# Pair products on one core: x in 16 KB rows, and four half stores in place of nine loads on GpSimd's DMA queue

## The chip, the cores and the metric

The kernel runs on one core of a Trainium2 chip. The metric is the time of one execution on the device in microseconds (us); it is given as the median of several runs. The core has a matrix engine (PE), a vector engine (DVE), a scalar engine (ACT), GpSimd (POOL) and a sync engine (SP); ACT, POOL and SP are used here only to issue DMA transfers, and all transfers run on the core's 16 DMA engines, numbered 0 to 15.

## The reference

The input holds 4096 samples of 32 fields with 64 numbers each. For each of the 496 pairs of fields (i, j) with i < j, field i is multiplied by a 64 x 64 matrix of that pair, and the result is multiplied element by element with field j. Everything is float32.

```python
i_idx, j_idx = np.triu_indices(32, k=1)
vi = inputs[:, i_idx, :]                       # (4096, 496, 64)
vj = inputs[:, j_idx, :]
vdotw = jnp.einsum('bpd,pde->bpe', vi, W)      # W: (496, 64, 64)
y = (vdotw * vj).reshape(4096, -1)
```

The output is 4096 x 31744 float32, 520 MB. The input x has 33.6 MB, the matrices W 8.1 MB.

## The kernel before, in words

**Tiling.** The samples are cut into 8 chunks of 512 (`NC` chunks of `BANK` columns). x is laid out transposed: a pair of fields p (16 of them, `NPR`) fills 128 partitions (two fields of 64) by 512 samples. Four pairs make a group (`GROUP`); the tile `x` holds all four groups of one chunk, 8 KB per partition and group. W stays in SBUF for the whole run.

**Steps.** `steps_of` lists the 124 steps of a chunk. A step (p, q) takes two PSUM banks: PE makes two blocks of 128 x 512 there (L190; the first step of a group, with q None, is four smaller matmuls, L181), and one DVE instruction multiplies them by the x rows of q and writes the two finished blocks into the ring (L207; L200 for the special step). Steps with p in group 0 come first, 55 of them, and begin with q in group 0, then group 1 from step 7, group 2 from step 23, group 3 from step 39; then follow 39 steps with p in group 1, 23 with p in group 2 and 7 with p in group 3. Over 8 chunks that makes 992 steps and 1984 blocks of 256 KB.

**Ring.** Finished blocks go into a ring of three slots of 20, 18 and 18 blocks (`SLOTS`). One filling of a slot is a turn; there are 107. When a slot is full, SP stores it (L216), 4608 or 5120 KB in 128 rows of 36 or 40 KB; in the first three turns each half is stored by itself. The slot may be filled again when its store has landed. The output tensor in DRAM has 128 long rows, one per partition, so the rows of one store lie 1984 x 2 KB = 4.06 MB apart.

**x loads.** Group g of the next chunk is loaded after the last step of the present chunk with p in g (`last`, L221 to L223), since nothing reads the old group after that. A load has 1 MB in 128 rows of 8 KB. Of the 32 loads, 23 are issued by ACT (L131).

**Nine loads on GpSimd.** The nine listed in `LIGHT_LOADS` are issued by GpSimd through `load_beside` (L105). A transfer from SP or ACT over 128 partitions gives each of the 16 DMA engines 8 rows. `load_beside` instead splits the load into two: rows 0 to 119 in 15 shares of 8 rows, which start at engine 5 and so leave out engine 4 (`LIGHT`), and rows 120 to 127 in two shares of 4 rows on two engines from `PAIRS_FROM`. [...] Before each of the two parts, `from_engine` therefore issues a tiny load into a tile `nudge` over as many engines as are needed to move on to the wanted one. The shares are kept apart in DRAM by pads of 16 numbers (`PAD`), so that the transfer has an outer dimension of 15 or 2. All of these stand in program order on GpSimd, which does nothing else.

Of the kernel before, what the change touches and what calls it, by code (L numbers as in the profile page):

```python
# [8 lines left out]
F32 = mybir.dt.float32  # L9
ALU = mybir.AluOpType  # L10

P = 128
BANK = 512
BANKS = 8

GROUP = 4
W_STEPS = [8, 16, 24, 32, 44]
SLOTS = [20, 18, 18]

DMA_ENGINES = 16  # L20
LIGHT = 4
LIGHT_LOADS = [(1, 0), (2, 0), (3, 0), (3, 2), (4, 0), (5, 0), (6, 0), (6, 2), (7, 0)]
PAIRS_FROM = [5, 7, 9, 11, 13, 15, 1, 6, 8]
HEAD = P // DMA_ENGINES
REST = HEAD // 2
PAD = 16


def steps_of(NPR):

    steps = []
    for g in range(0, NPR, GROUP):
        steps.append((g, None))
        for h in range(g, NPR, GROUP):
            for p in range(g, g + GROUP):
                steps += [(p, q) for q in range(max(h, p + 1), h + GROUP)]
    return steps


def row_half(p, i):  # L40

    return (i + p) % 2
# [10 lines left out]

def x_loads(B, NPR):

    return [(c, g) for c in range(B // BANK) for g in range(NPR // GROUP)]


def load_size(load, D):

    pads = (DMA_ENGINES + 1) * PAD if load in LIGHT_LOADS else 0
    return P * GROUP * BANK + pads


@with_exitstack
def pair_bilinear_kernel(
    ctx: ExitStack,
    tc: tile.TileContext,
    x: bass.AP,
    w: bass.AP,  # L70
    out: bass.AP,
    B: int,
    F: int,
    D: int,
):

    nc = tc.nc
    NC = B // BANK
    NPR = F // 2
    steps = steps_of(NPR)  # L80
    blocks = 2 * len(steps) * NC

    const = ctx.enter_context(tc.tile_pool(name="const", bufs=1))
    psum = ctx.enter_context(tc.tile_pool(name="ps", bufs=1, space=bass.MemoryType.PSUM))

    nudges = [const.tile([DMA_ENGINES, 16], F32, tag=f"nudge{i}", name=f"nudge{i}") for i in range(2)]
    cursor = 0

    def from_pool(out, in_):

        tc.keep_in_program_order(nc.gpsimd.dma_start(out=out, in_=in_))  # L91

    def from_engine(e):

        nonlocal cursor
        k = (e - cursor) % DMA_ENGINES
        if k:
            nudge = nudges[e == LIGHT + 1]
            from_pool(
                nudge[:k].rearrange("p (h c) -> p h c", h=2)[:, :, :4],  # L100
                x[: k * 8].rearrange("(p h c) -> p h c", p=k, h=2),
            )
        cursor = e

    def load_beside(at, xt, n_row, lap):  # L105

        nonlocal cursor
        most = DMA_ENGINES - 1
        for e, k, rows, p in (
            (PAIRS_FROM[lap], 2, REST, most * HEAD),  # L110
            (LIGHT + 1, most, HEAD, 0),
        ):
            from_engine(e)
            n = rows * n_row
            lines = x[at : at + k * (n + PAD)].rearrange("(k c) -> k c", k=k)
            from_pool(xt[p : p + k * rows], lines[:, :n])
            at += k * (n + PAD)
            cursor = (e + k) % DMA_ENGINES

    xbuf = const.tile([P, NPR * BANK], F32, tag="x", name="x")  # L120
    loads = x_loads(B, NPR)

    def load_x(load):

        at = sum(load_size(before, D) for before in loads[: loads.index(load)])
        n = GROUP * BANK
        xt = xbuf[:, ts(load[1], n)]
        if load in LIGHT_LOADS:
            load_beside(at, xt, n, LIGHT_LOADS.index(load))
        else:  # L130
            nc.scalar.dma_start(out=xt, in_=x[at : at + P * n].rearrange("(p c) -> p c", p=P))  # L131

    for g in range(NPR // GROUP):
        load_x((0, g))
    w_sb = const.tile([P, len(steps) * P], F32, tag="w", name="w")
    done = 0
    for n in W_STEPS:
        cols = slice(done * P, (done + n) * P)
        nc.sync.dma_start(out=w_sb[:, cols], in_=w[:, cols])
        done += n  # L140

    pring = psum.tile([P, BANKS * BANK], F32, tag="pring", name="pring")
    bank = 0

    def take_banks(n):

        nonlocal bank
        got = pring[:, bank * BANK : (bank + n) * BANK]
        bank = (bank + n) % BANKS
        return got  # L150

    ring = ctx.enter_context(tc.tile_pool(name="ring", bufs=1))
    made = base = stored = 0
    room = 0
    turn = -1

    def x_of(p, h=None):

        rows = slice(None) if h is None else slice(h * D, (h + 1) * D)
        return xbuf[rows, ts(p, BANK)]  # L160

    def strided(ap, step):

        return bass.AP(ap.tensor, ap.offset, [ap.ap[0], [step, 2], ap.ap[1]])

    for c in range(NC):
        for s, (p, q) in enumerate(steps):
            pm = take_banks(2)
            if made == base + room:
                turn += 1  # L170
                base, room = made, SLOTS[turn % len(SLOTS)]
                tag = f"slot{turn % len(SLOTS)}"
                osb = ring.tile([P, room * BANK], F32, tag=tag, name=tag)
            a = (made - base) * BANK
            for k in range(2):
                if q is None:
                    for h in range(2):
                        pair = p + 2 * k + h
                        m = row_half(pair, 2 * pair)
                        o = row_half(pair, 2 * pair + 1)  # L180
                        nc.tensor.matmul(  # L181
                            pm[o * D : (o + 1) * D, ts(k, BANK)],
                            w_sb[m * D : (m + 1) * D, s * P + k * D : s * P + (k + 1) * D],
                            x_of(pair, m),
                            start=True,
                            stop=True,
                        )
                else:
                    m = row_half(p, 2 * p + k)
                    nc.tensor.matmul(  # L190
                        pm[:, ts(k, BANK)],
                        w_sb[m * D : (m + 1) * D, ts(s, P)],
                        x_of(p, m),
                        start=True,
                        stop=True,
                    )
            if q is None:
                for h in range(2):
                    rows = slice(h * D, (h + 1) * D)
                    nc.vector.tensor_tensor(  # L200
                        strided(osb[rows, a : a + BANK], BANK),
                        strided(pm[rows, :BANK], BANK),
                        strided(x_of(p + 1 - h, h), 2 * BANK),
                        ALU.mult,
                    )
            else:
                nc.vector.tensor_tensor(  # L207
                    strided(osb[:, a : a + BANK], BANK),
                    strided(pm[:, :BANK], BANK),
                    strided(x_of(q), 0),  # L210
                    ALU.mult,
                )
            made += 2
            half = turn < len(SLOTS) and made - base == (room // 2 + 1) // 2 * 2
            if half or made in (base + room, blocks):
                nc.sync.dma_start(  # L216
                    out=out[:, stored * BANK : made * BANK],
                    in_=osb[:, (stored - base) * BANK : (made - base) * BANK],
                )
                stored = made  # L220
            last = s + 1 == len(steps) or steps[s + 1][0] // GROUP != p // GROUP  # L221
            if last and c + 1 < NC:
                load_x((c + 1, p // GROUP))  # L223


# [53 lines left out]
```

## Time and profile before

| | |
|---|---|
| median of 10 runs | 1316.0 us (1313.98 to 1317.82) |
| the profiled execution | 1316.78 us |
| its span, first to last instruction | 1314.6 us |
| bytes moved by DMA | 562.41 MB, of them 520.09 MB written to DRAM |
| stores of 4608 KB, SP | 68, median 24.8 us from issue to landing |
| stores of 5120 KB, SP | 35, median 24.4 us |
| x loads of 1024 KB, ACT | 23, median 18.5 us |
| x loads of 960 KB, GpSimd | 9, median 27.9 us |
| the rest of these, 64 KB, GpSimd | 9, median 12.7 us |
| nudges, GpSimd | 18 |

The profile is of one execution. Busy times are sums over an engine's instructions; idle time of an engine that isn't the bottleneck costs nothing. In the queue list, q1 carries what SP issues (stores and W), q10 what ACT issues, q0 what GpSimd issues, and q8 and q14 carry the engines' own instructions from DRAM. The time from issue to landing includes what stood in the queue ahead of the transfer. A packet is one row of a transfer[...].

### The profile page before, as it was taken

What the parts mean: (1) busy time and instruction counts of PE and PEld (TensorE: products, weight loads), DVE (VectorE), ACT (ScalarE), POOL (GpSimd) and SP (SyncE); (2) the same over time, 40 slices, a digit from 0 to 9 for tenths busy, and PEclk for the clock granted to TensorE, in tenths of its full rate; (3) what the DMA queues carried; (4) which work ended last, traced back from release to release, by engine and by line L of the source; (5) the groups of instructions that cost most, each with busy time, mean ns of one, the idle gap of its engine ahead of it and who ended that gap; (6) DMA issues with size and microseconds to landing.
All of it is one profiled execution on the core that took longest, in us unless ns stands there. A gap on an engine that the chain in (4) does not pass through costs nothing.

```text
span 1314.6 us, 9765 instructions
## 1 busy us (share of the span) xinstructions
PE 1133.3 (86%) x4096; PEld 337.9 (26%) x4096; DVE 1170.9 (89%) x1024; POOL 20.7 (2%) x40
## 2 busy tenths in 40 slices
PE   7988889898798887999889888798988988889991
PEld 2222222222222222222222222222222222222220
DVE  6998989999899987999889999799998989889993
POOL 0000000000000000000000000000000000000000
PEclk9999999999899999999889999899988989999996
DMA  9999999999999999999999999999999999999998
GB/s 391 431 433 431 430 436 432 432 432 428 437 430 433 430 429 427 429 428 432 431 432 428 433 426 431 433 432 417 436 426 429 436 425 434 427 434 431 430 435 354
DMA packets 22507, 562.41 MB, mean 428 GB/s; under 512 B 3648, under 2 KB 3648, under 8 KB 3776
## 3 DMA queue, kind: packets, MB, share of 16 engines
q1 hardware_dynamic: 16560, 528.23, 93.5%
q10 hardware_dynamic: 3312, 24.12, 4.4%
q0 software_dynamic: 2592, 9.45, 1.8%
q8 instruction: 32, 0.52, 0.1%
q14 instruction: 11, 0.09, 0.0%
HBM read 41.69 MB, written 520.09 MB: 427 GB/s over the span
## 4 chain that ended last, share of the span: by engine, by line
DMA 65%; DVE 31%; PE 1%; issue 1%; DVEq 0%
DMA out_dram<-slot 64%; DVE slot L207 29%; DVE slot L200 2%; PE pring L190 1%; DMA x<-in_x_dram 1%; PE pring L181 0%; DVEq L207 0%; DVEq L269 0%; DVEq L200 0%
## 5 line engine op out<-in xcount | busy, mean ns | idle before, releaser
L190 PE MATMUL pring<-x,w 64*128 64x512 f32 x3840 | 1072.2, 657 | 146.3 <-DVE slot L207 106.7
L207 DVE TENSOR_TENSOR slot<-pring,x 128x1024 f32<-128x1024 f32 x960 | 1095.2, 1213 | 106.5 <-DMA out_dram<-slot 101.6
L190 PEld LDWEIGHTS pring<-x,w 64*128 64x128 f32 x3840 | 322.5, 194 | 896.2 <-DVE slot L207 753.6
L200 DVE TENSOR_TENSOR slot<-pring,x 64x1024 f32<-64x1024 f32 x64 | 77.9, 1217 | 14.8 <-PE pring L181 11.5
L181 PE MATMUL pring<-x,w 64*64 64x512 f32 x256 | 63.5, 615 | 9.3 <-DMA x<-in_x_dram 7.6
L181 PEld LDWEIGHTS pring<-x,w 64*64 64x64 f32 x256 | 15.4, 135 | 53.9 <-DVE slot L207 27.2
L91 POOL DMA_DIRECT2D x<-in_x_dram x18 | 10.5, 585 | 1022.6 <-PE pring L190 1022.6
L91 POOL DMA_DIRECT2D nudge<-in_x_dram x18 | 10.1, 562 | 0.9 <-POOLq L265 0.9
L265 POOL MEMSET const-float32-0.0<- 128x1 f32 x1 | 0.1, 98 | 0.2 <-issue 0.2
L265 POOL MEMSET const-bfloat16-1.0<- 128x1 bf16 x1 | 0.1, 101 | 0.0
L265 POOL MEMSET const-uint8-127<- 128x1 uint8 x1 | 0.1, 99 | 0.0
L265 POOL MEMSET const-float32-1.0<- 128x1 f32 x1 | 0.1, 98 | 0.0
## 6 DMA issues: line engine op xcount, KB each, us to landing
out_dram<-slot SPq DMA_DIRECT2D x68, 4608.0 KB, 24.8
out_dram<-slot SPq DMA_DIRECT2D x35, 5120.0 KB, 24.4
x<-in_x_dram ACTq DMA_DIRECT2D x23, 1024.0 KB, 18.5
out_dram<-slot SPq DMA_DIRECT2D x4, 2560.0 KB, 22.2
x<-in_x_dram POOLq DMA_DIRECT2D x9, 960.0 KB, 27.9
out_dram<-slot SPq DMA_DIRECT2D x2, 2048.0 KB, 23.0
w<-in_w_dram SPq DMA_DIRECT2D x1, 2816.0 KB, 25.3
w<-in_w_dram SPq DMA_DIRECT2D x1, 2048.0 KB, 23.1
```

The lines of the kernel that those rows point to most:

```text
L91: tc.keep_in_program_order(nc.gpsimd.dma_start(out=out, in_=in_))
L181: nc.tensor.matmul(pm[o * D : (o + 1) * D, ts(k, BANK)], w_sb[m * D : (m + 1) * D, s * P + k * D : s * P + (k + 1) * D], x_of(pair, m), st ...
L190: nc.tensor.matmul(pm[:, ts(k, BANK)], w_sb[m * D : (m + 1) * D, ts(s, P)], x_of(p, m), start=True, stop=True,)
L200: nc.vector.tensor_tensor(strided(osb[rows, a : a + BANK], BANK), strided(pm[rows, :BANK], BANK), strided(x_of(p + 1 - h, h), 2 * BANK), A ...
L207: nc.vector.tensor_tensor(strided(osb[:, a : a + BANK], BANK), strided(pm[:, :BANK], BANK), strided(x_of(q), 0), ALU.mult,)
L265: nc = bacc.Bacc("TRN2", target_bir_lowering=False, num_devices=1)
```

## The change

Four things change together.

1. x is loaded for two groups at once, 2 MB in 128 rows of 16 KB, except for the first two loads of chunk 0, which stay at one group each. `x_loads` now lists (chunk, first group, end group). For a later chunk, groups 0 and 1 are loaded after the last step with p in group 1, and groups 2 and 3 after the last step with p in group 3.
2. ACT issues all 17 x loads. `LIGHT_LOADS`, `PAIRS_FROM` and `load_beside` are gone, and so are the pads in x.
3. In turns 18, 45, 71 and 98 (`LIGHT_TURNS`) the slot is stored in two halves. The first, 10 blocks, is issued by GpSimd through `store_beside`: partitions 0 to 119 in 15 shares from engine 5 on, and partitions 120 to 127 in k shares from engine e on, with (e, k) from `REST_ON`: engines 7 and 8; 15, 0, 1 and 2; 15 and 0; 1 and 2. The second half, 10 or 8 blocks, is issued by SP.
4. The output in DRAM is no longer 128 long rows. Each store writes one contiguous region, partition after partition; the shares of the four GpSimd stores have pads of 16 numbers between them. The host puts the blocks in order.

```diff
-LIGHT_LOADS = [(1, 0), (2, 0), (3, 0), (3, 2), (4, 0), (5, 0), (6, 0), (6, 2), (7, 0)]
-PAIRS_FROM = [5, 7, 9, 11, 13, 15, 1, 6, 8]
+LIGHT_TURNS = [18, 45, 71, 98]
+REST_ON = [(7, 2), (15, 4), (15, 2), (1, 2)]
 HEAD = P // DMA_ENGINES
-REST = HEAD // 2
+MOST = DMA_ENGINES - 1
 PAD = 16
...
 def x_loads(B, NPR):
-    return [(c, g) for c in range(B // BANK) for g in range(NPR // GROUP)]
+    loads = [(0, 0, 1), (0, 1, 2), (0, 2, 4)]
+    for c in range(1, B // BANK):
+        loads += [(c, 0, 2), (c, 2, 4)]
+    return loads
+
+def stores_of(blocks):
+    stores = []
+    made = turn = 0
+    while made < blocks:
+        room = SLOTS[turn % len(SLOTS)]
+        half = (room // 2 + 1) // 2 * 2
+        cuts = [half, room - half] if turn < len(SLOTS) or turn in LIGHT_TURNS else [room]
+        for i, n in enumerate(cuts):
+            n = min(n, blocks - made)
+            if n:
+                light = LIGHT_TURNS.index(turn) if i == 0 and turn in LIGHT_TURNS else None
+                stores.append((made, n, light))
+                made += n
+        turn += 1
+    return stores
+
+def store_parts(store):
+    at, n, light = store
+    if light is None:
+        return [(0, 1, P)]
+    e, k = REST_ON[light]
+    return [(MOST * HEAD, k, HEAD // k), (0, MOST, HEAD)]
...
-    def load_beside(at, xt, n_row, lap):
+    def store_beside(at, osb, light):
         nonlocal cursor
-        most = DMA_ENGINES - 1
-        for e, k, rows, p in (
-            (PAIRS_FROM[lap], 2, REST, most * HEAD),
-            (LIGHT + 1, most, HEAD, 0),
-        ):
+        n = osb.shape[-1]
+        for e, (p, k, rows) in zip((REST_ON[light][0], LIGHT + 1), store_parts((0, n // BANK, light))):
             from_engine(e)
-            n = rows * n_row
-            lines = x[at : at + k * (n + PAD)].rearrange("(k c) -> k c", k=k)
-            from_pool(xt[p : p + k * rows], lines[:, :n])
-            at += k * (n + PAD)
+            m = rows * n
+            lines = out[at : at + k * (m + PAD)].rearrange("(k c) -> k c", k=k)
+            from_pool(lines[:, :m], osb[p : p + k * rows])
+            at += k * (m + PAD)
             cursor = (e + k) % DMA_ENGINES
...
-        if load in LIGHT_LOADS:
-            load_beside(at, xt, n, LIGHT_LOADS.index(load))
-        else:
-            nc.scalar.dma_start(out=xt, in_=x[at : at + P * n].rearrange("(p c) -> p c", p=P))
+        n *= g1 - g0
+        xt = xbuf[:, g0 * GROUP * BANK : g0 * GROUP * BANK + n]
+        nc.scalar.dma_start(out=xt, in_=x[at : at + P * n].rearrange("(p c) -> p c", p=P))
...
-            half = turn < len(SLOTS) and made - base == (room // 2 + 1) // 2 * 2
-            if half or made in (base + room, blocks):
-                nc.sync.dma_start(
-                    out=out[:, stored * BANK : made * BANK],
-                    in_=osb[:, (stored - base) * BANK : (made - base) * BANK],
-                )
-                stored = made
+            at, n, light = stores[0]
+            if made == at + n:
+                part = osb[:, (at - base) * BANK : (made - base) * BANK]
+                if light is None:
+                    nc.sync.dma_start(
+                        out=out[stored : stored + P * n * BANK].rearrange("(p c) -> p c", p=P),
+                        in_=part,
+                    )
+                else:
+                    store_beside(stored, part, light)
+                stored += store_size(stores.pop(0))
             last = s + 1 == len(steps) or steps[s + 1][0] // GROUP != p // GROUP
-            if last and c + 1 < NC:
-                load_x((c + 1, p // GROUP))
+            for load in loads:
+                if last and load[0] == c + 1 and load[2] == p // GROUP + 1:
+                    load_x(load)
```

`store_size` gives the number of elements that a store takes in DRAM, its pads included. The matmuls and the DVE instructions are the same, in the same order.

## The prediction

> **What bounds the kernel now.** I read the page's busy shares, slices and queues first, then the chain of waits, the groups, the waits, a table of windows, and last the DMA activity of the final 35 us.
>
> ```profile
> span 1314.6 us, 9765 instructions
> PE 1133.3 (86%) x4096; PEld 337.9 (26%) x4096; DVE 1170.9 (89%) x1024; POOL 20.7 (2%) x40
> DMA  9999999999999999999999999999999999999998
> DMA packets 22507, 562.41 MB, mean 428 GB/s; under 512 B 3648, under 2 KB 3648, under 8 KB 3776
> q1 hardware_dynamic: 16560, 528.23, 93.5%
> q10 hardware_dynamic: 3312, 24.12, 4.4%
> q0 software_dynamic: 2592, 9.45, 1.8%
> q8 instruction: 32, 0.52, 0.1%
> q14 instruction: 11, 0.09, 0.0%
> DMA 65%; DVE 31%; PE 1%; issue 1%; DVEq 0%
> L207 DVE TENSOR_TENSOR slot<-pring,x 128x1024 f32<-128x1024 f32 x960 | 1095.2, 1213 | 106.5 <-DMA out_dram<-slot 101.6
> ```
>
> DVE and PE are near the span, yet DVE's idle time ends on a store 101.6 us long: it waits for ring slots. The chain is 65% store DMA and only then DVE. The windows table says how full the DMA is (columns: window, then busy time and count of PE, PEld, DVE, POOL, then granted clock, DMA share, GB/s):
>
> ```profile
> 35.00:100.00 65.00, 58.69 (x210) 17.54 (x210) 60.18 (x54) 2.25 (x4) 0.95 1.01 433
> 100.00:500.00 400.00, 349.94 (x1280) 103.38 (x1276) 363.94 (x319) 6.75 (x12) 0.97 1.00 431
> 900.00:1290.00 390.00, 347.22 (x1256) 103.24 (x1252) 359.52 (x316) 4.01 (x7) 0.96 1.00 431
> 1290.00:1315.00 25.00, 0.00 (x0) 0.00 (x0) 2.23 (x2) 0.00 (x0) 0.52 0.75 322
> ```
>
> From 35 to 1290 us no DMA engine has a gap, so only three things can shorten the kernel: fewer bytes or packets, fewer stretched packets, or a tail in which the 16 engines stop together. The tail, in 40 slices of 0.875 us from 1280 to 1315 us:
>
> ```profile
> DMA  9879699699599798998999979999895735320000
> GB/s 590 379 337 590 295 463 548 295 463 506 253 590 426 342 613 346 407 445 365 510 421 421 562 328 421 421 431 431 346 477 225 328 169 225 150 94 37 19 0 0
> ```
>
> It fades over eight slices, 7 us. The packet records behind these views (start, duration, size, queue) make this exact: an engine's next packet starts 3 to 4 ns before its last one ends, so records link into 16 chains. By where those chains stop, the first engine ends 7.1 us before the last, and the mean 3.7 us before it. Perfect balance would be worth 3.7 us.
>
> Who is late can be told from the same chains. Each of the 32 instruction packets (q8, 16 KB, every 40 us) holds one engine 0.92 us and stretches that engine's next packet by 0.40 us: 1.32 us together. They return to the same engine every eighth time, so eight engines pay 4 x 1.32 = 5.3 us each and eight none. The chains that carry 12 instead of 8 rows of a GpSimd load name the engines: those paying are 5, 6 and 9 to 14. Engine 3 carries most of q14's 8 KB packets (about 4 us, an estimate from their 0.31 us plus a similar stretch). One chain has no rows of the GpSimd loads, so it is engine 4; its large packets take 1378 to 1396 ns where all others take 1364, and 30 ns x 847 such packets is 25 us over the run. Engine 4 is slow, and the nine GpSimd loads spare it 9 x 8 rows x 305 ns = 22.0 us.
>
> [...] the 18.5 us of a 1 MB x load agree: 8 rows x (305 + 1360) = 13.3 us and 5.2 us fixed.
>
> **The change, part by part.** Time per packet from link to link: 8 KB 305, 16 KB 607, 20 KB 757, 36 KB 1360, 40 KB 1510 ns, 4 B 6 ns.
>
> *x in 16 KB rows.* 4096 rows x 305 = 1249.3 us become 256 x 305 + 1920 x 607 = 1243.5; over 16 engines -0.36 us. Small packets: GpSimd's 36 DMAs left 1440, the new 16 leave about 640 (32 each plus nudges), ACT's completions fall by 96; 900 x 6 ns / 16 = -0.34 us. Four more turns cut in half: 512 rows x 4 ns / 16 = +0.13 us. Sum -0.57 us.
>
> *Later loads.* Groups 0-1 are now asked for after step 94 of 124, first read 30 steps on, PE four steps sooner: 26 x 1.21 = 31 us. Groups 2-3 are asked for at a chunk's end and first read (by DVE) at step 23: 28 us. A 2 MB load needs 8 x (607 + 1360) + 5.2 = 20.9 us: hidden. The longest ACT load of before took 31.2 us; if that recurs DVE stalls some 6 us, but two stores (12 us each) stand queued whenever DVE gets a slot and one is left when it has filled it, so the engines stay busy; beyond 12 us each us counts. ACT queues nothing but these loads.
>
> *Light stores.* In turns 18, 45, 71 and 98 GpSimd issues nudge, rest, nudge and 15 shares; SP issues the second half. GpSimd waits for DVE with nothing but its own later DMAs behind it, and SP loses one wait. Eight light rows per engine, about eight small packets between, alternate with queued SP rows: 16 x 1.36 + 8 x 0.757 + 5 = 33 us to land, against 24.8 for a whole store. SP's rows are pushed back at most 6 us; the same bytes flow, the 12 us of backlog covers it, and DVE gains back 12.1 - 11.4 = 0.7 us per turn over 26 turns. Cost zero, up to +1 us at each if the cover is thinner.
>
> *Balance.* The light stores spare engine 4 by 4 x 8 x 757 = 24.2 us. The rests fall on 7, 8 (4 + 4 rows, 6.1 us) and 15, 0, 1, 2 (2 + 4 rows, 4.5 us), the very engines without instruction packets. Extra work per engine, us:
> Before: 6 and 9: 5.3 + 8 rows x 0.305 = 7.7; 5, 10 to 14: 6.5; 7, 8: 2.4; 15, 0, 1, 2: 1.2; 3: 4; 4: 25.4 - 22.0 = 3.4. Mean 4.5, most 7.7: the last is 3.2 behind the mean (3.7 measured, so the count holds to 0.5).
> After: 5, 6, 9 to 14: 5.3; 7, 8: 6.1; 15, 0, 1, 2: 4.5; 3: 4; 4: 1.2. Mean 4.9, most 6.1: 1.2 behind.
> Gain 2.0 us; between 0 (the remaining scatter replaces it) and 2.5.
>
> *Stretched packets.* While GpSimd's x loads ran in the second half, packets beyond their usual times add 33 engine-us, and 15 ACT loads 11; on ACT the nine would cost about 7. Saved up to 26 / 16 = 1.6 us, or nothing if it hangs on addresses, which all change. I take 0.6.
>
> *Output layout.* Rows that stood 3.9 MB apart become contiguous. Before shows no contiguous store, but contiguous x loads run at full packet speed: I take 0. The pads of the first light store (17 x 64 B) put every later row 64 B or more off a 256 B boundary. [...] In before, x rows after the first light load are off by 64 B too and take 309 ns, as aligned ones do. [...] I take 0.
>
> Sum: -0.57 - 2.0 - 0.6 = -3.2 us. The profiled execution took 1316.8 us (span 1314.6 and 2.2 around it); it would give 1313.6. It stands 0.8 above the median of 1316.0, whose forecast is 1312.8.
>
> **Rivals.**
> *Balance doesn't improve.* For it: engine 4's slowness swings (14 to 47 ns per packet), so 24.2 us may spare it wrongly, and skew grows between four large corrections instead of nine small ones. Against: the eight-fold rhythm of the instruction packets is strict and PE's program is unchanged. Leaves -0.57 and little more: 1315.4.
> *Offset rows cost.* Some 89 turns x 8 = 712 rows per engine [...] It cancels the gain at 4.5 ns a row and is slower by over 0.2% from 8.1. For it: no aligned or offset store can be compared in before. Against: the reads.
> *A starved ring.* 2 MB loads or light stores open gaps in the DMA: 0.9 us per chunk over seven chunks is +6.3, 1319.1. For: DVE fills a slot only 6% faster than it drains. Against: 12 us of backlog.
>
> **How the numbers follow.** 0.2%, about what a measurement tells from no change, is 2.6 us. Forecast 1312.8: 0.55 (own range 1311 to 1315; 0.46 of it faster, 0.09 same). Balance: 0.23 (0.02 faster, 0.21 same). Offset rows: 0.14 (0.12 slower, 0.02 same). Starved ring: 0.08 (0.06 slower, 0.02 same). So faster 0.48, same 0.34, slower 0.18. The range runs from 1310.4 (all upper savings: 0.57 + 2.5 + 1.6, and 1 us of scatter) to 1318.6, leaving half of the slower cases out.
>
> **What would show it.** Right: a tail that fades over 3 us, not 7; no GpSimd x loads; DMA share 1.00 in the middle windows; 36 KB packets still at 1364 ns. Wrong: those packets at 1370 or more after turn 18 (offset rows); DMA share under 1.00 after a chunk's end or a light turn, with DVE waiting for x (starved ring); a tail as long as before (balance).

## The result, and the profile after

The changed kernel takes 1347.8 us (median of 8 runs, 1346.7 to 1349.5) against 1316.2 (29 runs by then): a ratio of 1.0242, with a 95% interval of 1.0233 to 1.0251. It is 31.6 us slower. The forecast was 1312.8, and the range ended at 1318.6.

The page of the changed kernel (slices: 40 of 33.7 us; queues: packets, MB, share of 16 engines):

```profile
span 1346.6 us, 9693 instructions
PE 1134.6 (84%) x4096; PEld 344.8 (26%) x4096; DVE 1170.6 (87%) x1024; POOL 9.3 (1%) x20
DMA  9999999999999999999999999999999999999997
GB/s 391 430 436 431 436 433 431 368 424 430 427 428 429 433 428 433 429 374 407 427 431 432 433 425 426 432 402 401 410 409 432 432 430 429 429 429 389 395 411 305
q1 hardware_dynamic: 16560, 517.74, 90.6%
q10 hardware_dynamic: 2448, 33.56, 5.9%
q0 software_dynamic: 1120, 10.49, 2.5%
L237 DVE TENSOR_TENSOR slot<-pring,x 128x1024 f32<-128x1024 f32 x960 | 1095.0, 1213 | 141.0 <-DMA out_dram<-slot 135.7
```

PE and DVE work as long as before. The DMA engines look as busy as before, but the rate falls in four places, which begin at slices 8, 18, 27 and 37. Each begins with one of the four turns that have a GpSimd store. Slices 29, 30 and 39 come after such a turn; there the DMA share is 0.95 to 0.99, so some engines stand idle. Also q0 moves 10.49 MB in 2.5% of the span where it moved 9.45 MB in 1.8%. In windows around the first of these turns (window, busy time and count of PE, PEld, DVE, POOL, clock, DMA share, GB/s), the changed kernel shows

```profile
170.00:235.00 65.00, 56.27 (x200) 17.34 (x200) 57.45 (x51) 1.80 (x4) 0.92 1.00 431
235.00:265.00 30.00, 25.25 (x96) 8.07 (x92) 25.31 (x23) 0.41 (x1) 0.94 1.00 361
265.00:300.00 35.00, 27.75 (x102) 9.56 (x104) 30.25 (x27) 0.00 (x0) 0.90 1.01 424
```

and the kernel before, which has a GpSimd load at 236 us, shows in the second of these windows

```profile
235.00:265.00 30.00, 25.53 (x96) 7.17 (x92) 26.79 (x25) 2.25 (x4) 0.97 1.00 430
```

The share is 1.00 in both, but the rate is 361 against 430 GB/s: the packets take longer, none are missing. The DMA view of the changed kernel from 225 to 300 us, in slices of 1.9 us, shows how long it lasts:

```profile
DMA  8998999999998999999999999999999999999999
GB/s 374 452 433 374 511 422 404 444 415 435 380 382 273 326 295 317 350 306 306 350 374 369 454 413 433 472 393 452 433 413 461 404 426 520 391 393 415 347 402 452
```

That is 12 slices, some 22 us, at 273 to 382 GB/s. The packet records (start, duration, size, queue) divide the whole difference. Two sums are needed: the work (packet times less their 4 ns overlap, averaged over 16 engines) and the idle time (first packet to last, less the work).

| us, mean of 16 engines | before | changed | difference |
|---|---|---|---|
| stretch in the four light turns | 0 | 19.5 | +19.5 |
| stretch beside x loads | 5.2 | 6.8 | +1.6 |
| stretch elsewhere | 2.2 | 5.5 | +3.3 |
| all work | 1306.6 | 1330.5 | +23.9 |
| idle, the tail included | 4.8 | 12.7 | +7.9 |
| sum | 1311.4 | 1343.2 | +31.8 |

"Stretch" is what packets take beyond the usual time of their size. How the second and third row divide depends on where the time of a load is taken to begin; together they are +4.9. The rest of the work differs by -0.5 us, as forecast for rows and small packets. The question was why a 20 KB row of a GpSimd store, 761 ns at full speed, takes 1041 ns on average and up to 2866, and why SP's rows beside it grow too.

### The profile page after: what moved, and what is told of

Same layout as the page of the kernel before. It is cut to its first block, busy times and chain, and to the rows that moved or that the text cites. A ratio compares the mean times of both kernels' runs of the same rounds, so it can differ in the third digit from the quotient of the medians.

```text
span 1346.6 us, 9693 instructions
## 1 busy us (share of the span) xinstructions
PE 1134.6 (84%) x4096; PEld 344.8 (26%) x4096; DVE 1170.6 (87%) x1024; POOL 9.3 (1%) x20
## 3 DMA queue, kind: packets, MB, share of 16 engines
q0 software_dynamic: 1120, 10.49, 2.5%
## 4 chain that ended last, share of the span: by engine, by line
DMA 63%; DVE 32%; PE 2%; issue 1%; DVEq 0%; POOL 0%
DMA out_dram<-slot 63%; DVE slot L237 29%; DVE slot L230 3%; PE pring L220 2%; PE pring L211 1%; DMA x<-in_x_dram 1%; DVEq L237 0%; DVEq L299 0%; POOL out_dram L123 0%; POOL nudge L123 0%
## 5 line engine op out<-in xcount | busy, mean ns | idle before, releaser
L220 PEld LDWEIGHTS pring<-x,w 64*128 64x128 f32 x3840 | 329.3, 196 | 922.1 <-DVE slot L237 764.3
L123 POOL DMA_DIRECT2D out_dram<-slot x8 | 4.7, 583 | 1217.4 <-DVE slot L237 1217.4
L123 POOL DMA_DIRECT2D nudge<-in_x_dram x8 | 4.6, 569 | 0.9 <-POOLq L295 0.9
## 6 DMA issues: line engine op xcount, KB each, us to landing
out_dram<-slot POOLq DMA_DIRECT2D x4, 2400.0 KB, 32.8
```

The source lines that it names most:

```text
L220: nc.tensor.matmul(pm[:, ts(k, BANK)], w_sb[m * D : (m + 1) * D, ts(s, P)], x_of(p, m), start=True, stop=True,)
```

## The experiments

Four theories. Theory 1: it matters which engine reads a partition. When a GpSimd share is read by another engine than the one that reads these partitions in SP's stores, both take longer. (No trace names the partitions that an engine reads. own_ports below is the placement that theory 1 takes to match SP's stores: an engine's own partitions are those that it has there, and a row on any other engine is crossed.) Theory 2: two store streams, or stores from GpSimd, stretch each other anyway. Theory 3: contiguous regions in DRAM are to blame. Theory 4: leaving out an engine is.

**1. The same quarters, on their own engines and crossed.** Both kernels are the changed one with four quarters of 32 partitions per light half, 8 shares of 4 rows each. They differ in the engine a quarter starts on, and in the one nudge that takes it there.

```diff
-REST_ON = [(7, 2), (15, 4), (15, 2), (1, 2)]
+QUARTERS = [(0, 0), (64, 8), (32, 0), (96, 8)]   # own_ports: (first partition, first engine)
+QUARTERS = [(0, 8), (64, 0), (32, 8), (96, 0)]   # crossed_ports
...
-    return [(MOST * HEAD, k, HEAD // k), (0, MOST, HEAD)]
+    return [(p, 8, 4) for p, e in QUARTERS]
```

> The changed kernel, but the four GpSimd half stores go out as four quarters of 32 partitions, 8 shares of 4 rows each, [...] (0-31 and 32-63 on engines 0-7, 64-95 and 96-127 on 8-15); no engine is left out. Theory 1 [...]: the stretch of about 5 us per engine and turn is gone, DMA rate in the four turns stays above 420 GB/s; but engine 4, 25 us slow, is no longer spared and stays some 20 us behind: 1330 to 1337 us. Theory 2 (two store streams to DRAM, or stores from GpSimd as such, stretch each other wherever their rows come from): rate in these turns falls to about 330 GB/s as in the changed kernel, 1347 us or more.

> The same four quarters, each on the other eight engines (partitions 0-31 and 32-63 on engines 8-15, 64-95 and 96-127 on 0-7), after one nudge: the same bytes, rows and DMAs. Theory 1: [...] the stretch of the changed kernel is back, rate in the four turns near 330 GB/s, and the time is 12 to 20 us above own_ports: 1345 to 1355. Theory 2: the same time as own_ports within 2 us.

Measured: own_ports 1329.5 us (ratio 1.0105, 1.0091 to 1.0119), crossed_ports 1349.0 (1.0253, 1.0239 to 1.0267). Windows of own_ports before, in the first and around the second light turn:

```profile
100.00:235.00 135.00, 115.57 (x420) 35.45 (x416) 119.48 (x106) 1.96 (x4) 0.95 1.00 431
235.00:265.00 30.00, 25.37 (x94) 7.93 (x92) 25.67 (x23) 0.32 (x1) 0.94 1.00 428
570.00:610.00 40.00, 37.22 (x135) 9.93 (x132) 37.38 (x34) 0.00 (x0) 1.00 0.98 422
```

The same windows of crossed_ports:

```profile
100.00:235.00 135.00, 116.15 (x416) 36.48 (x416) 119.08 (x106) 1.92 (x4) 0.92 1.00 431
235.00:265.00 30.00, 25.13 (x94) 8.58 (x92) 25.19 (x23) 0.22 (x1) 0.89 1.02 345
570.00:610.00 40.00, 28.16 (x104) 8.95 (x100) 28.59 (x26) 1.24 (x3) 0.90 1.00 365
```

Same bytes, rows, DRAM regions, queue and number of stores; 428 against 345 GB/s in the first turn, 422 against 365 in the second. In the third and fourth light turn own_ports shows

```profile
890.00:930.00 40.00, 35.96 (x128) 9.63 (x128) 38.71 (x34) 0.00 (x0) 1.00 0.94 405
1220.00:1260.00 40.00, 35.18 (x126) 11.54 (x128) 35.55 (x33) 0.00 (x0) 0.91 0.95 406
```

and crossed_ports

```profile
890.00:930.00 40.00, 30.77 (x108) 9.65 (x108) 30.17 (x27) 2.12 (x4) 0.91 1.00 375
1220.00:1260.00 40.00, 30.42 (x106) 9.22 (x106) 31.77 (x29) 2.12 (x4) 0.88 1.01 396
```

So own_ports misses the 420 GB/s that I expected in all four turns, but its packets aren't longer: the share of 0.94 and 0.95 says that engines stand idle. Linked to 16 chains, the packets show 15 engines idle for some 5 to 11 us in the run, and for 0.7 us the one with slow 36 KB rows, engine 4, which is behind the others (experiment 4).

In the records 476 of own_ports' 512 light rows take 761 to 764 ns and none over 794. In crossed_ports only 206 do, a tenth take 1555 ns or more, twice 761, and SP's rows grow by 36 to 78 us per turn, summed over the engines. Stretch in the four turns: 0.3 us against 22.3, mean of the engines. Why some crossed rows run at full speed wasn't shown; which row met which wasn't tried. Theory 2 falls.

crossed_ports has one nudge, of 8 shares, at the start of the run (5.6 us to landing), own_ports has none, and all four turns differ, also the last two (405 against 375 GB/s, 406 against 396). This fits what `cursor` counts: the shares of a GpSimd DMA begin on the engine after the last one of the DMA before.

**2. Half the dose.** Only the second pair of quarters is crossed.

```diff
-QUARTERS = [(0, 0), (64, 8), (32, 0), (96, 8)]
+QUARTERS = [(0, 0), (64, 8), (32, 8), (96, 0)]
```

> own_ports with the second pair of quarters crossed: partitions 0-31 and 64-95 on the engines that own them, 32-63 on engines 8-15 and 96-127 on 0-7, after a nudge. Theory 1 [...], as a dose: half the crossed rows, half the loss between own_ports (1329.5) and crossed_ports (1349.0): 1337 to 1341 us, some 11 us of stretch averaged over the engines. If the loss were one of being out of step at all, and not of the crossed rows, it would stand near 1349.

Measured: 1340.7 us (1.0189, 1.0172 to 1.0206), stretch 7.5 us in the light turns: the time as expected, the stretch smaller than the 11 us expected. That the time fits is partly luck: of the 11.1 us from own_ports' first to last packet to this kernel's, 6.9 are work, and 4.2 are more idle time (19.8 against 15.6 us). Windows around the first two light turns:

```profile
235.00:265.00 30.00, 25.62 (x96) 6.94 (x92) 25.50 (x23) 1.71 (x4) 1.00 1.01 409
...
570.00:610.00 40.00, 31.55 (x111) 10.86 (x110) 31.14 (x28) 0.55 (x1) 0.87 0.98 402
```

Both rates lie between those of experiment 1.

**3. The layout alone.** The kernel before, each store written as one region.

```diff
-                    out=out[:, stored * BANK : made * BANK],
+                    out=out[P * stored * BANK : P * made * BANK].rearrange("(p c) -> p c", p=P),
```

> The kernel before with one part of the change: each store writes one contiguous region. Theory 1 (layout costs nothing): 1316 us, within 1.5. Theory 3 (contiguous stores collide with x loads or with each other in DRAM; the packets beside x loads were stretched about three times as much in the changed kernel): 1320 us or more, with stretched packets in the windows of x loads.

Measured: 1315.9 us (0.9998, 0.9990 to 1.0006). Theory 3 falls; contiguous regions cost nothing and gain nothing. (The diff leaves out the tensor's shape and the host's part.)

**4. Engine 4 without relief.** nolight is the kernel before with `LIGHT_LOADS = []`; sp_halves is the changed kernel with `light = None` for every store, so that SP issues all of them.

> The kernel before with no light loads: ACT issues all 32 x loads, nothing spares engine 4. My reading (engine 4 is 25 us slow and the light loads spare it 22): it falls some 17 us further behind the mean, 1329 to 1334 us, and the tail is one engine working alone. If engine 4 isn't slow by itself: 1316 us.

> The changed kernel with the four half stores issued by SP as plain stores over 128 partitions: no GpSimd DMA at all, everything else as changed. Theory 1: the same as own_ports, 1329.5 within 2 us[...]. Theory 2: clearly faster than own_ports.

Measured: nolight 1328.2 us (1.0089, 1.0075 to 1.0103), sp_halves 1329.0 (1.0096, 1.0082 to 1.0110). So the kernel before takes 12 us longer if nothing spares engine 4, 1 less than the lower end of what I expected. By the packet sums, 9.4 of them are idle time (14.2 against 4.8 us) and 2.4 are work. The last 35 us of nolight:

```profile
DMA  9909909909110997909099390909961010100000
GB/s 590 632 42 674 632 42 674 632 42 674 42 84 42 702 463 323 702 42 744 0 744 609 140 749 0 749 0 468 468 281 47 0 47 0 47 9 28 19 19 0
```

From slice 31 the rate is 47 and 0 in turn: one engine with one row at a time. It is the chain with the slow 36 KB rows, 1387 ns, so engine 4. And own_ports against sp_halves is 0.5 us: half stores from GpSimd cost next to nothing on their own engines.

**5. Engine 4 left out, shares on their own engines.** own_shares puts partitions 0-19 and 32-51 on engines 0 to 3, 20-31 and 52-63 on 5 to 7, the rest as in own_ports, with one-element nudges to step over engine 4. own_shares2 replaces these.

```diff
-REST_ON = [(7, 2), (15, 4), (15, 2), (1, 2)]
...
+SHARES = [                                 # own_shares: partition, engine, shares, rows in a share
+    (0, 0, 4, 5), (20, 5, 3, 4), (64, 8, 8, 4),
+    (32, 0, 4, 5), (52, 5, 3, 4), (96, 8, 8, 4),
+]
+SHARES = [                                 # own_shares2
+    (20, 6, 2, 6), (64, 8, 8, 4), (0, 0, 4, 5),
+    (52, 6, 2, 6), (96, 8, 8, 4), (32, 0, 4, 5),
+]
```

> The changed kernel with its four GpSimd half stores regrouped: engine 4 is still left out (its partitions 16-19 and 48-51 go with others on engines 0 to 3, 5 rows each), [...] (20-31 and 52-63 on 5 to 7, 64-95 and 96-127 on 8 to 15). Theory 1 [...] together with a slow engine 4: no stretch to speak of, 420 GB/s or more in the four turns, no lone engine at the end: 1315 to 1320 us. If leaving out an engine is what stretches packets (theory 4): about 330 GB/s there and 1340 us or more.

> own_shares with its cursor put right: the one-element nudge is replaced, partitions 20-31 and 52-63 go in two shares of 6 rows to engines 6 and 7, so engine 4 gets no light row [...]. Theory 1: stretch of about a quarter of crossed_ports' 22 us, 4 to 7 us. Eight DMAs from GpSimd per turn land as late as in own_shares (38 us), so the ring starves again, by some 50 us in all: 1360 to 1380 us. If skipping an engine stretches packets by itself: 15 us of stretch or more.

own_shares: 1399.3 us (1.0633, 1.0616 to 1.0649), 79 us above the upper end of its forecast; stretch 17.1 us. It didn't try what it was meant to: no chain is without light rows, and the counts of its first turns (about three of 10, one of 5, one of 4) fit a one-element nudge after which the next DMA began where it would have begun without it, so that nearly every share after the first was crossed. own_shares2: 1395.2 us in one run, with 32 of the 128 light rows of a turn crossed; stretch 4.8 us, as expected for a quarter. Its shares of 6 rows leave out engine 5 as well as 4, and two chains have no light rows. In its first light turn, eight chains have the 8 light rows that only engines 8 to 15 get, all on their own engines: none of their packets, light or SP's, is stretched at all. The two chains without light rows have nothing crossed, yet their SP rows grow by 1.4 and 4.8 us in this turn and by 4.4 to 5.3 in the last two, while other engines have light rows of their partitions. So the stretch isn't only on the engine with the crossed row. Theory 4 falls.

Both are slow for another reason, and own_shares2 came 15 to 35 us above its forecast. DVE in own_shares2 around the first light turn (start, length, what; in brackets the idle time before and what ended it):

```profile
251.79 10.27 DVE L237 TENSOR_TENSOR slot<-pring,x 128x1024 f32<-128x1024 f32 x9 [1.62 <-DMA out_dram<-slot]
286.56 24.98 DVE L237 TENSOR_TENSOR slot<-pring,x 128x1024 f32<-128x1024 f32 x22 [24.49 <-DMA out_dram<-slot]
```

and its windows there:

```profile
235.00:265.00 30.00, 25.33 (x94) 6.96 (x92) 25.40 (x23) 2.84 (x5) 1.00 1.00 423
265.00:305.00 40.00, 17.15 (x62) 6.26 (x64) 18.44 (x17) 0.00 (x0) 0.66 0.57 241
```

Of the 512 light rows, 431 take 761 to 764 ns, and the first window still has 423 GB/s. But eight DMAs per turn leave many small packets in q0, 2048 in the run against 768 in own_ports, and the chains of the first turn alternate: one packet of q0, then one row of SP, 36 KB for the most part, so that nearly every small packet waits for a row. The parts land after 30 to 39 us, the slot comes free late, DVE waits 24.5 us, and the DMA engines run dry: share 0.57. This is the starved ring of my third rival, in a kernel that I made.

**6. The first part of the change alone, and the balance alone.** x16_lightloads is the kernel before with x in 16 KB rows and four light loads of 2 MB; pairs is the kernel before with other engines for rows 120 to 127.

```diff
-LIGHT_LOADS = [(1, 0), (2, 0), (3, 0), (3, 2), (4, 0), (5, 0), (6, 0), (6, 2), (7, 0)]
-PAIRS_FROM = [5, 7, 9, 11, 13, 15, 1, 6, 8]
+LIGHT_LOADS = [(1, 0, 2), (3, 0, 2), (5, 0, 2), (7, 0, 2)]  # x16_lightloads
+PAIRS_FROM = [7, 15, 1, 7]
... (x_loads as in the changed kernel, and what follows from it)
```

```diff
-PAIRS_FROM = [5, 7, 9, 11, 13, 15, 1, 6, 8]
+PAIRS_FROM = [7, 15, 1, 7, 15, 1, 7, 15, 1]                # pairs
```

> The kernel before with the first part of the change alone: x in 16 KB rows, four of these 2 MB loads light (groups 0-1 of chunks 1, 3, 5, 7; rests on 7-8, 15-0, 1-2, 7-8), the old output layout. Theory 1 (loads write SBUF while stores read it, so crossed shares don't collide): no stretch in the light loads, 1315.5 within 1.5. If crossed shares collide in loads too: 2 MB of them cost some 4 us each, 1325 or more.

> The kernel before with one list changed: rows 120 to 127 of the nine light loads go only to the engines without instruction packets (7-8, 15-0, 1-2, three times each). My balance step: extra work falls from at most 7.7 to 5.3 us on the last engine with the mean unchanged at 4.6, so 2.4 us faster, 1313.6 us, and a tail that fades over some 3 us. If the balance step is wrong: 1316 us.

x16_lightloads: 1314.9 us (0.9992, 0.9985 to 0.9998), the lowest median of all kernels here, 1.2 us under the one before and no clear gain. Its windows:

```profile
100.00:500.00 400.00, 351.54 (x1266) 102.31 (x1266) 361.57 (x317) 4.54 (x8) 0.95 1.00 430
500.00:900.00 400.00, 355.47 (x1276) 103.03 (x1272) 363.89 (x320) 2.26 (x4) 0.96 1.00 431
900.00:1290.00 390.00, 345.83 (x1246) 101.88 (x1244) 358.98 (x315) 1.71 (x3) 0.96 1.00 432
```

No dip. Its light shares are crossed as those of the changed kernel are, but they write SBUF while SP's stores read it; stretch is 5 to 18 us in each of the four loads, summed over all engines, against 73 to 86 in each light turn of the changed kernel. pairs: 1315.6 us (0.9998, 0.9990 to 1.0006), no gain.

## Why the prediction was wrong, point by point

**What bounds the kernel: right.** The DMA engines set the time of the changed kernel too: their work and idle time account for the difference.

**Light stores: wrong, the step that failed.** "Cost zero, up to +1 us at each if the cover is thinner." I priced their effect on the order of stores and took the speed of a row as given, 757 ns. The runs show a mean of 4.9 us of stretch per engine and turn, 19.5 in all, and experiment 1 shows that it comes from the crossed rows: 0.3 us in all without them. (The 15 shares landed after 32.8 us, against the 33 worked out; as that sum had no stretch in it, this is chance.) The trace of before held no case of it: there, the crossed shares were loads, and I carried their full speed (8 KB in 309 ns) over to stores. In the first turn, shares placed as in own_ports run at 428 GB/s, the same shares on the other eight engines at 345; and of the changed kernel's 128 light rows per turn none is on the engine that own_ports gives it. What in the hardware makes the placement matter wasn't shown.

**Balance: the slow engine is real, the gain isn't shown.** Not sparing engine 4 costs 12 us. Of the 2.0 us for moving the rests nothing was measured: pairs alone was to bring 2.4 and brought between +1.3 and -0.8 us. The profiled run of before, which I read the 3.7 us tail from, was one of 1316.8 us; contig's, with the same loads on the same engines, has 4.0 us of mean idle time against 4.8 in before, and pairs' 3.5. So the tail itself differs between executions by part of what I meant to gain; what else takes it wasn't settled. In the changed kernel engine 4 was spared, but that gained nothing: at the end its chain (36 KB rows of 1396 ns) stops 7.7 us before the last packet, and another engine, whose last 31 such rows take 1368 ns and follow each other without a gap, works on alone. Of the 12.7 us of mean idle time, some 9 fall in the last 70 us, where the others wait for slots and stop early. This fits a stretch that fell unevenly on the engines, and put another one behind; what each engine lost wasn't told apart, as some links between packets are ambiguous. In crossed_ports, which spares none, engine 4 is the last, and takes only 1.2 us more. That the two have nearly the same idle time (12.7 and 12.9 us) is chance as far as is known.

**Rows and small packets: right,** -0.5 us for -0.57. On each chain an SP or ACT transfer leaves 8 rows and one 4 B packet: in the records of before, 8 rows stand between two such packets in 1457 of the 1459 stretches whose links are unambiguous. ACT's 4 B packets fell from 368 to 272, and GpSimd's small ones from 1440 to 608. (In the balance step, engine 4 has 824 rows of 36 and 40 KB, not 847; the 25 us stand.)

**Stretched packets: wrong sign.** I took -0.6 for x on ACT; the changed kernel shows +1.6 beside the loads. It doesn't come with 16 KB rows: x16_lightloads has them and as much stretch in all as the kernel before, to 0.2 us, while nolight has 5.9 us with rows of 8 KB alone, and sp_halves 5.7. Both of these have an engine far behind, as the changed kernel has; whether that is the cause wasn't tried.

**Later loads: right.** No DVE wait on an x load is listed after the start, and the 2 MB loads landed after 21.0 us, against 20.9 worked out. That sum takes ACT's rows to alternate with SP's: of 3111 unambiguous links from a packet of q10 in before, 11 lead to another one of q10.

**Output layout: right for regions, wrong for offset rows.** The regions cost nothing by experiment 3. The rows off a multiple of 256 B do cost something, about 3 ns for one of 36 KB (table). The pads of the first two light stores come to 17 and 19 times 64 B, together 2304 B, a multiple of 256; so rows are off in turns 18 to 45 and from 71 on, and not in every later turn, as I wrote. Mean time of SP's 36 KB rows, those over 1420 ns left out:

| ns | 300 to 570 us | 640 to 890 us | 960 to 1225 us |
|---|---|---|---|
| before | 1365.8 | 1365.9 | 1365.6 |
| changed | 1368.9 (off) | 1365.7 | 1368.5 (off) |
| crossed_ports | 1365.7 | 1365.5 | 1365.7 |

The pads of crossed_ports and own_ports come to 2048 B per turn, so their SP rows stay on a multiple. After the fourth light store of the changed kernel the rows stand 128 B off, and from 1270 us on the mean is 1367.3. With about 3 ns for a 36 KB row, 4 for one of 40 KB and some 500 such rows per engine, the price is some 1.7 us, an estimate from these means. It is part of the +3.3 us of stretch elsewhere; the rest of that is open.

**The rivals.** None was the one that came. Offset rows were there, with an estimated 1.7 us. The ring didn't starve in the light turns (DMA share 0.99 to 1.00 in windows of all four). The chance of 0.18 for slower had neither the mechanism nor the size.

## What to carry to other kernels

A DMA's speed wasn't a property of its size and queue alone. Where two transfers ran at once and both read SBUF, it mattered which engine had which partitions: 428 against 345 GB/s for own_ports and crossed_ports; so a split is worth trying in both placements. A split that shifts rows to other engines, to relieve a slow one, did no harm where loads ran beside stores (x16_lightloads, 1314.9 us). And more DMAs on a queue that alternates with long rows landed later: the parts of own_shares2 after 30 to 39 us with eight DMAs per turn, those of own_ports after 21.4 with four. The short ring felt that (DVE waited 24.5 us around the first light turn) with the same bytes to store.

## What else the runs showed of the hardware

Engine 4 needs 1378 to 1396 ns for a 36 KB store packet where the others need 1364, in every kernel here in which it could be told apart; why wasn't tried. In before the 32 instruction packets of 16 KB (q8) fall on the same eight engines in turn and cost 1.32 us each. A GpSimd DMA of one element did not move on the engine at which the next one begins, as far as the row counts of own_shares tell (about three chains of 10, one of 5, one of 4). And stretch isn't in proportion to the crossed rows: 0.3, 4.8, 7.5 and 22.3 us for none, a quarter, half and all of 128; these kernels also differ in the order and size of their shares.
